# Another order of the weight transfers, and of the first small products, in a fused CIN kernel

## The chip, the cores and the metric

The kernel runs on one core of a Trainium2 chip. The metric is the device time of one execution in microseconds (us), as the median of several runs. The core has five engines that run side by side: TensorE (PE in the profile, PEld its weight loads), VectorE (DVE), ScalarE (ACT), GpSimd (POOL) and SyncE (SP), which only issues transfers. Sixteen DMA engines carry the transfers that ACT, SP and POOL issue.

## The reference

```python
B, F, E = (1024, 39, 64)      # of x as it is given; HID = [64, 64, 64]
def _cin_layer(Xk, X0, W, b):
    O = W.shape[0]
    Hk, Fdim = (Xk.shape[1], X0.shape[1])
    Wr = W.reshape(O, Hk, Fdim)
    return jnp.einsum('bhe,bfe,ohf->boe', Xk, X0, Wr) + b[None, :, None]
X0 = sparse_embedding
Xk = X0
outs = []
for W, b in ((W0, b0), (W1, b1), (W2, b2)):
    Xk = _cin_layer(Xk, X0, W, b)
    outs.append(Xk.sum(axis=-1))
cin_output = jnp.concatenate(outs, axis=-1)
return cin_output @ fc_w.T + fc_b
```

Three layers, each a product of all pairs of fields (39 of x with 39 or 64) with a weight matrix, summed at the end to one number for each of the 1024 rows.

## The kernel before, in words

Only the first layer is computed as it stands. The output needs no more of layers two and three than sums over the embedding axis with fc, and these are linear in the weights. So W2 and the last third of fc are put together into a small matrix V2 (`v2` in the code), and V2 with W1 into a second set of columns beside W0. One big product per block then gives both, and the end result is a product of the two, summed.

**The main loop.** x is cut in 32 blocks of 32 rows (2048 columns). For a block POOL gathers the fields in five arrangements (`roll`, L174) out of a table in DRAM (`xd`), VectorE multiplies pairs of arrangements (`product`, L219, six for a block, and a small one, L221, for two blocks), and TensorE multiplies each by the weights of its chunk (`multiply`, L561; `join`, L581 and L592 for the small one). ScalarE and VectorE finish a block (L604 to L622). VectorE runs four chunks ahead of TensorE.

**The start**, which the change is about, must do two things before that loop:

*Weights.* TensorE turns fc's row into columns, by products of one row with a single one (`turn`, L323): `turn_twice` with a doubled row that POOL writes (`fcrow2`, L320) and `turn_row` straight from fc's row. Both write columns of one PSUM tile, `small`. VectorE makes `fc2` of column 0 (L357). Then on TensorE, in this order: W2 with `fc2` (L403), two small products that double the result (L435, `spread_v2`), seven transposes of W0 (L415, `turn_w0`), and W1 with V2 in four groups (L484). In between VectorE transposes L403's result (L422) and writes V2 (L448, L455). ScalarE copies the turned W0 (L461) into `both`, VectorE transposes L484's four results (L493), and ScalarE and VectorE copy them to `both` as well (L500, L503). From `both`, `weight_rows` takes the sums for one chunk (L526, L528), `weight_turn` transposes them on TensorE (L545) and ScalarE writes them to `wa` (L546, L547), whose columns the main product loads. There are eight chunks; the first four are made before the loop, the rest inside it.

*Rows of x.* The first block doesn't come out of the table: two halves of x are loaded by themselves (`xh`, L252), and eight gathers read them (L389), four arrangements for each half. Behind the sixth POOL issues the load of block 1 (L168). SP copies both halves to the table (L393), and a ninth gather takes the fifth arrangement from there.

**What sets the order.** Each engine runs its instructions in the order in which they are written; there is no scheduler. ACT issues W2, x's first half, W0, W1 and x's second half on its own queue, one behind the other, ahead of all its other work. Between TensorE's products stand spins (`spin`, L279), products of constants that nobody reads; they keep TensorE at work.

Of the kernel before, what the change touches and what calls it, by code (L numbers as in the profile page):

```python
# [60 lines left out]
B, F, E, H = 1024, 39, 64, 64  # L61
# [14 lines left out]
MM = 512  # L76
# [71 lines left out]
def cin_kernel(ctx: ExitStack, tc: tile.TileContext, x, w0t, b0, w1, b1, w2, b2, fc_w, fc_b, out):  # L148
    nc = tc.nc
# [75 lines left out]
    with prep as prep:  # L225
        w2s = prep.tile([128, FH // 2], F32, name="w2s")
        w1s = prep.tile([128, FH // 2], F32, name="w1s")
        w0s = prep.tile([NW * F, NF * H], F32, name="w0s")
        flat = prep.tile([128, 4, NA, 32], F32, name="flat")
        fcrow = prep.tile([1, 3 * H], F32, name="fcrow")  # L230
# [20 lines left out]
        def load_half(k):  # L251
            nc.scalar.dma_start(  # L252
                xh[k].rearrange("f (b e) -> b f e", e=E), x[k * SB : (k + 1) * SB]
            )

        nc.scalar.dma_start(w2s, w2.rearrange("o (s n) -> (o s) n", s=2))
        load_half(0)
        nc.scalar.dma_start(w0s, w0t.rearrange("b (s a) h -> (b s) (a h)", s=NW))
        nc.scalar.dma_start(w1s, w1.rearrange("o (s n) -> (o s) n", s=2))
        load_half(1)  # L260
        nc.gpsimd.iota(place, pattern=[[0, 1]], base=0, channel_multiplier=1)
        nc.gpsimd.iota(apart, pattern=[[1, 128]], base=0, channel_multiplier=-1)
# [14 lines left out]
        def spin(n=1, cols=MM // 2):  # L277
            for _ in range(n):
                nc.tensor.matmul(  # L279
                    idle[:, 0:cols],  # L280
                    nc.const_aps.tensor(1.0, (128, 128), F32),
                    nc.const_aps.tensor(1.0, (128, cols), F32),
                    start=True,
                    stop=True,
                )

        spin(1, MM)


        tmp = prep.tile([128, 16], F32, name="tmp")  # L290
# [31 lines left out]
        def turn(dst, row):  # L322
            nc.tensor.matmul(dst, row, one, start=True, stop=True)  # L323

        def turn_row(h, at, row, k):
            turn(small[h : h + H, at : at + 1], row[:, k * H : k * H + H])

        def turn_twice(at, row, k):
            turn(small[:, at : at + 1], row[:, k].rearrange("p h s -> p (h s)"))
# [6 lines left out]
                nc.gpsimd.memset(steps_by[:, k, i : i + 1], float(by))  # L336
        bothv = both.rearrange("p (a b) -> p a b", b=FT)
        nc.gpsimd.memset(bothv[0:H, :, F], 0.0)
        for at, k in ((0, 1), (6, 0)):
            turn_twice(at, fcrow2, k)  # L340
        spin(1, 3 * MM // 4)

        nc.vector.tensor_copy(row, place)
        step(row, F, 1.0, j)
# [151 lines left out]
        for k, a in groups:  # L496
# [4 lines left out]
            if k > 1:  # L501
# [4 lines left out]
                    ),  # L506
                    flat[0:H, first, new:, 0 : FT - 32],
                )
        spin(1, MM)
        for h in (0, H):  # L510
            turn_row(h, 1, fcrow, 0)
        turn_row(0, 2, fcrow, 2)
        spin(1, MM)
        first = [prods.tile([128, BLK], F32, name="p", tag="p") for _ in range(3)]


# [164 lines left out]
    n, c = steps[3]  # L681
# [9 lines left out]
    for at, (n, c) in enumerate(steps[:-TAIL]):  # L691
# [30 lines left out]
        if at + AHEAD < len(steps):  # L722
            n, c = steps[at + AHEAD]
# [84 lines left out]
```

## Time and profile before

| what | value |
|---|---|
| median of 3 runs | 734.01 us (733.33 to 734.38) |
| the profiled execution, its own time | 733.53 us |
| span of the profile (first to last instruction) | 731.5 us |
| bytes read from HBM, written | 196.76 MB, 10.60 MB |
| main product L561: 1536 passes, busy | 665.2 us |
| first pass of the main product | at 17.40 us of the span |

TensorE takes an f32 product in two passes, so each matmul of the code stands twice in the profile. The times in the timeline count from the start of the span; a group of instructions of one line stands there with the start of its first and the time until its last ends. What a timeline names in brackets is the idle time of that engine ahead of the instruction, and the event that came last before it; with waits for several events it can be another one that ended the wait.

The shares by stage, the first instructions of the weights' and rows' paths and their waits are shown in the prediction.

### The profile page before, as it was taken

How to read it: one execution, taken by the hardware profiler on the slowest of the kernel's cores; microseconds unless marked ns; L12 is line 12 of the kernel's file. 1: busy time of each engine (PE TensorE's matmuls, PEld its weight loads, DVE VectorE, ACT ScalarE, POOL GpSimd, SP SyncE). 2: the span in 40 equal slices, each digit the busy share in tenths (PEclk: the TensorE clock that was granted, in tenths of full speed). 3: DMA queues.
4: the chain of work that ended last, by engine and by line, in shares of the span. 5: the costliest groups of instructions: out<-in, count | busy, mean ns of one | idle time of the engine just before them, and what ended most of it. 6: DMA issues, size and time to landing. Idle time of an engine off the chain costs nothing.

```text
span 731.5 us, 6359 instructions
## 1 busy us (share of the span) xinstructions
PE 726.7 (99%) x2379; PEld 315.3 (43%) x2379; DVE 638.2 (87%) x521; ACT 167.0 (23%) x240; POOL 401.0 (55%) x254
## 2 busy tenths in 40 slices
PE   9999999999999999999999999999999999999998
PEld 4444444444444444444444444444444444444443
DVE  6989699988889988889988889888898988889885
ACT  3332121222212222121222212222121221212222
POOL 6779869636555445754537555455654547545300
PEclk9999999999999999999999999999999999999999
DMA  8986796989575787757679575886767777566700
GB/s 273 378 322 251 304 367 247 382 324 366 219 283 222 284 339 279 277 226 280 273 288 326 230 280 222 310 345 233 280 244 278 299 287 280 197 267 234 288 0 1
DMA packets 65983, 197.24 MB, mean 270 GB/s; under 512 B 40110, under 2 KB 40179, under 8 KB 45984
## 3 DMA queue, kind: packets, MB, share of 16 engines
q0 software_dynamic: 28784, 185.56, 64.9%
q1 hardware_dynamic: 35468, 9.29, 5.5%
q10 hardware_dynamic: 1700, 1.99, 0.9%
q8 instruction: 18, 0.29, 0.2%
q14 instruction: 13, 0.11, 0.0%
HBM read 196.76 MB, written 10.60 MB: 283 GB/s over the span
## 4 chain that ended last, share of the span: by engine, by line
PE 87%; DVE 5%; issue 3%; DMA 2%; POOL 2%; ACT 0%; DVEq 0%; POOLq 0%
PE po L561 80%; PE po L581 4%; DVE p L219 3%; PE po L592 2%; POOL r L174 2%; DVE g L611 1%; DMA r<-xd,lists 1%; DMA b0s<-in_b 1%; PE idle L279 1%; DVE sums L622 1%; DVE pairs L528 0%; PE pv L403 0%; PE pt L484 0%; PE pw L415 0%; PE pv L484 0%
## 5 line engine op out<-in xcount | busy, mean ns | idle before, releaser
L561 PE MATMUL po<-p,wa 128*128 128x512 f32 x1536 | 665.2, 593 | 0.6 <-DVE p L219 0.5
L219 DVE TENSOR_TENSOR p<-r 128x2048 f32<-128x2048 f32 (+2 forms) x198 | 433.8, 2223 | 72.8 <-PE po L561 63.8
L174 POOL DMA_INDIRECT r<-xd,lists x156 | 316.3, 2028 | 264.4 <-issue 255.0
L561 PEld LDWEIGHTS po<-p,wa 128*128 128x128 f32 x1536 | 289.7, 190 | 371.9 <-issue 353.7
L609 ACT ACTIVATE z<-po,columns 64x512 f32<-64x512 f32 x128 | 87.4, 683 | 374.2 <-PE po L592 216.0
L611 DVE SCALAR_TENSOR_TENSOR g<-po,b0s,z 64x512 f32<-64x512 f32 x128 | 95.9, 749 | 9.3 <-ACT z L609 5.3
L604 ACT COPY g<-r 39x1024 f32<-39x1024 f32 x64 | 66.7, 1043 | 161.5 <-DVE sums L622 129.7
L622 DVE TENSOR_REDUCE sums<-g 103x16 f32<-103x1024 f32 x62 | 75.6, 1219 | 2.1
L174 POOL DMA_INDIRECT u<-xd,lists x16 | 40.1, 2509 | 7.1 <-issue 4.6
L581 PE MATMUL po<-p,wa 32*64 32x512 f32 x512 | 31.6, 600 | 0.0
L174 POOL DMA_INDIRECT v<-xd,lists x16 | 26.5, 1659 | 4.9 <-issue 4.9
L221 DVE TENSOR_TENSOR p<-u,v 128x1024 f32<-128x1024 f32 x16 | 19.5, 1216 | 0.0
L581 PEld LDWEIGHTS po<-p,wa 32*64 32x64 f32 x512 | 9.4, 131 | 20.1 <-issue 20.1
L592 PE MATMUL po<-u,wa 32*64 32x512 f32 x256 | 17.0, 587 | 0.0
L174 POOL DMA_INDIRECT r<-xh,lists x8 | 8.0, 1002 | 4.7 <-DVE tmp L384 2.6
L592 PEld LDWEIGHTS po<-u,wa 32*64 32x64 f32 x256 | 5.8, 132 | 8.1 <-issue 8.0
L279 PE MATMUL idle<-const-float32-1.0 128*128 128x512 f32 (+2 forms) x12 | 7.7, 732 | 0.8 <-PEq L795 0.8
L528 DVE TENSOR_TENSOR pairs<-both 128x2 f32<-128x2 f32 (+27 forms) x59 | 6.1, 172 | 0.3
L546 ACT COPY wa<-tr 128x128 f32<-128x128 f32 x8 | 2.1, 266 | 15.3 <-PE tr L545 15.3
L279 PEld LDWEIGHTS idle<-const-float32-1.0 128*128 128x128 f32 x12 | 2.5, 253 | 1.9 <-issue 1.7
L168 POOL DMA_DIRECT2D xd<-in_x x3 | 3.2, 1056 | 0.0
L461 ACT COPY both<-pw 64x468 f32<-64x468 f32 (+2 forms) x4 | 1.9, 472 | 4.4 <-issue 4.3
(97 smaller groups left out, 55.2 us busy)
## 6 DMA issues: line engine op xcount, KB each, us to landing
xd<-in_x SPq DMA_DIRECT2D x28, 312.0 KB
r<-xd,lists POOLq DMA_INDIRECT x156, 9.1
xd<-in_x POOLq DMA_DIRECT2D x3, 312.0 KB
w2s<-in_w ACTq DMA_DIRECT2D x1, 624.0 KB
w1s<-in_w ACTq DMA_DIRECT2D x1, 624.0 KB
w0s<-in_w0t ACTq DMA_DIRECT2D x1, 380.2 KB
xh<-in_x ACTq DMA_DIRECT2D x2, 156.0 KB
xd<-xh SPq DMA_DIRECT2D x2, 156.0 KB
```

The source lines that it names most:

```text
L174: nc.gpsimd.indirect_dma_start(dst, None, table, bass.IndirectOffsetOnAxis(ap=lists[:, k : k + 1], axis=0))
L219: nc.vector.tensor_tensor(p[:, cols], r[:, i, cols], r[:, k, cols], ALU.mult)
L221: nc.vector.tensor_tensor(p[:, 0:SUB], ut[n // 2 % 2], vt[n // 2 % 2], ALU.mult)
L279: nc.tensor.matmul(idle[:, 0:cols], nc.const_aps.tensor(1.0, (128, 128), F32), nc.const_aps.tensor(1.0, (128, cols), F32), start=True, sto ...
L528: nc.vector.tensor_tensor(out, diagonal(a, b, sa, sb), diagonal(b, a, sb, sa), ALU.add)
L561: nc.tensor.matmul(po[n][m], wa[:, c, side : side + 2 * H], p[:, bass.ts(m, MM)], start=n % 2 == 0 and c == 0, stop=n % 2 == 1 and c == NP ...
L581: nc.tensor.matmul(dst[half * H : half * H + H], wa[rows, NPAIR, at : at + H], p[rows, bass.ts(side, MM)], start=t >= 2, stop=t < 2 and ha ...
L592: nc.tensor.matmul(dst[half : half + H], wa[rows, NPAIR + 1, H : 2 * H], ut[n // 2 % 2][rows, bass.ts(side, MM)], start=False, stop=t < 2,)
L604: nc.scalar.copy(gt[H : H + F], rt[n % 2][0:F, 0, bass.ts(m, SUB)])
L609: nc.scalar.activation(z[one], po[n][m][other], AF.Identity, bias=fc0s[other])
L611: return lambda: nc.vector.scalar_tensor_tensor(g[n][m // 2][0:H, at], po[n][m][one], b0s[one], z[one], ALU.add, ALU.mult)
L622: nc.vector.tensor_reduce(sums[:, b_at : b_at + SB], g[n][m // 2].rearrange("p (b e) -> p b e", e=E), AX.X, ALU.add,)
```

## The change

ACT issues its transfers in the order W2, W1, x's first half, W0, x's second half. The first spin has 256 columns instead of 512. All five turns of fc's row now stand ahead of L403: two of `turn_row` that only read fc's row come first, then the two of `turn_twice`, then the last `turn_row`. The spin behind them has 128 columns instead of 384. After L484 the three `turn_row` are gone and the two spins of 512 columns that stood around them come one after the other. In the new kernel lines from about L290 on are numbered differently, by -1 to +3. No other instruction is added or taken away on any engine.

```diff
         nc.scalar.dma_start(w2s, w2.rearrange("o (s n) -> (o s) n", s=2))
+        nc.scalar.dma_start(w1s, w1.rearrange("o (s n) -> (o s) n", s=2))
         load_half(0)
         nc.scalar.dma_start(w0s, w0t.rearrange("b (s a) h -> (b s) (a h)", s=NW))
-        nc.scalar.dma_start(w1s, w1.rearrange("o (s n) -> (o s) n", s=2))
         load_half(1)
...
-        spin(1, MM)
+        spin()
...
+        for h in (0, H):
+            turn_row(h, 1, fcrow, 0)
         for at, k in ((0, 1), (6, 0)):
             turn_twice(at, fcrow2, k)
-        spin(1, 3 * MM // 4)
+        turn_row(0, 2, fcrow, 2)
+        spin(1, MM // 4)
...
-        spin(1, MM)
-        for h in (0, H):
-            turn_row(h, 1, fcrow, 0)
-        turn_row(0, 2, fcrow, 2)
-        spin(1, MM)
+        spin(2, MM)
```

## The prediction

> **What bounds the kernel now.** First the engines' busy time on the page, then stretches of the span, then the timeline of its first 30 us.
>
> ```profile
> PE 726.7 (99%) x2379; PEld 315.3 (43%) x2379; DVE 638.2 (87%) x521; ACT 167.0 (23%) x240; POOL 401.0 (55%) x254
> ```
>
> TensorE is busy 726.7 of 731.5 us. A busy TensorE need not run at its peak, so I went through the starts of its matmuls one after the other: from 20.75 us a 512-column pass starts every 0.43 us up to the end of the main product, and the only later gap over 0.15 us is one of 0.62 us at 101.02. The steady part is TensorE's own and the change leaves it alone. What can move is when the main product (L561) starts, at 17.40, and whether it then stalls.
>
> In this view the columns are stretch, length, busy time of PE, PEld, DVE, ACT, POOL, clock, mean share of the 16 DMA engines, GB/s:
>
> ```profile
> 5.00:9.00 4.00, 4.00 (x13) 1.44 (x14) 2.72 (x17) 1.11 (x2) 1.58 (x2) 1.00 0.93 275
> 9.00:13.00 4.00, 4.00 (x16) 3.15 (x17) 1.61 (x9) 2.21 (x5) 3.09 (x4) 1.00 0.98 278
> 13.00:17.40 4.40, 4.23 (x18) 1.90 (x16) 3.80 (x17) 2.16 (x9) 3.48 (x5) 1.00 0.98 352
> 17.40:30.00 12.60, 12.43 (x31) 5.29 (x32) 12.27 (x42) 4.05 (x15) 8.30 (x6) 1.00 1.01 375
> 30.00:44.00 14.00, 14.00 (x77) 5.80 (x76) 12.26 (x23) 4.37 (x21) 10.50 (x10) 1.00 1.01 391
> ```
>
> The DMA engines are full from about 5 to 44 us. So a transfer here is paid for by every later one, and DMA time lost early is not made up before 44 us. VectorE has 12.27 of 12.60 us in the stretch from 17.40 to 30.
>
> From the timeline (start, duration, then in brackets the idle time before and its releaser):
>
> ```profile
> 5.34 2.40 PE L403 MATMUL pv<-w2s,fc 128*64 128x320 f32 x8
> 7.11 1.05 POOL L174 DMA_INDIRECT r<-xh,lists  x1 [2.60 <-DVE tmp L384]
> 8.82 0.62 PE L435 MATMUL pv<-blocks,twice 64*128 64x20 f32 x4
> 9.38 1.63 PE L415 MATMUL pw<-unit,w0s 117*128 117x117 f32 x7
> 10.79 2.36 PE L484 MATMUL pt<-w1s,v 128*128 128x320 f32 x4
> ...
> 17.40 1.12 PE L561 MATMUL po<-p,wa 128*128 128x512 f32 x2 [0.17 <-issue]
> ...
> 23.06 2.45 DVE L219 TENSOR_TENSOR p<-r 128x1024 f32<-128x1024 f32 x2 [0.32 <-DMA r<-xh,lists]
> ...
> 28.70 0.79 DVE L528 TENSOR_TENSOR pairs<-both 128x22 f32<-128x22 f32 x7
> ...
> 29.66 0.27 PE L545 MATMUL tr<-unit,pairs 128*128 128x128 f32 x1
> ```
>
> The trace's semaphore records say when each transfer of ACT's queue had landed: W2 4.78, x's first half (xh0) 6.24, W0 8.69, W1 9.94, x's second half (xh1) about 10.1. Against these:
> - POOL's first gather is put down to "DVE tmp L384", but POOL's own wait on xh0 ends at 6.27 and the gather starts 0.84 later: xh0 is what it waits for. The next seven follow at some 1.24 us each.
> - At 23.06 DVE waits 0.32 for gathered rows, those of L389's seventh gather, landed at 23.04.
> - From there DVE has no gap until its sums for the fifth chunk end at 29.50, and the transpose waiting for them loads at 29.55, which is just when TensorE is ready for it. So 23.04 is on the path already, with about 0.1 us of slack.
> - W0 (8.69) is ready before L415 (9.38), and W1 (9.94) before L484 (10.79): neither is waited for.
>
> **What the skill says.** The Trainium skill, "DMA: Bandwidth & Descriptors", section "Queues, rings and completion order", says each DMA engine takes the descriptors of one issuer's ring in ring order. The trace agrees: the landings above are in issue order. "Issuing engines are not separate DMA queues" on the same page says that transfers from ACT, SP and POOL share the 16 engines; here POOL's gathers show it by taking 4.6 us from start to landing for the first and 7.2 us for the fifth to seventh, as the engines fill. "TensorE: Matmul & The Clock Gate", "What's actually happening", says that TensorE starts at half clock and is let go after a busy window of about 3.4 us whose phase is not tied to the kernel. Here passes of L484 start 0.53 us apart up to 12.95 and 0.29 to 0.33 apart after it, so the clock came at about 13.0.
>
> **The change, part by part.**
>
> 1. *W1 ahead of xh0, W0 and xh1.* ACT's five issues (0.41, 0.63, 0.83, 0.36, 0.55 us) only change places, and end at 3.65 as before. W1 lands some 3 us earlier, at about 6.6, and nobody gains: L484 stands behind L415 on TensorE, whose order is unchanged. W1 is 128 packets of 4,992 B at 0.19 to 0.24 us, on 16 engines 8 x 0.21 = 1.7 us. That goes ahead of xh0: 6.24 + 1.7 = 7.9, and ahead of W0.
>
> 2. *W0.* Its last data packet ended at 7.85, and W1 then took the engines to 9.48. In the new order W0 ends where W1 did, 9.3 to 9.5; its semaphore came 0.46 (W1) to 0.84 us (W0) after the last data, so it lands at 9.8 to 10.3. L415 moves from 9.38 to about 9.9 to 10.4, and with it L484, the transposes of its result, the weights and the start of L561: +0.5 to +1.0, I take 0.7.
>
> 3. *The gathers.* First gather at 7.9 + 0.9 = 8.8 instead of 7.11, so +1.7 for all eight and for the load that POOL issues among them at 14.38. On the DMA engines: the first gathered packet came 1.8 us after issue (8.9), so now about 10.6. ACT's transfers, which shared their last 1.2 us with 64 gather packets of 0.16 us (64 x 0.16 / 16 = 0.64 us, up to 0.8 with their longer packets), end at about 9.35 instead of 10.08. The engines so stand idle from 9.35 to 10.6, 1.25 us. A gather is 128 x 0.16 / 16 = 1.27 us of engine time against 1.24 us of issue: nothing catches up. The seventh gather lands at 23.04 + 1.25 = 24.3. SP's copies of x to the table wait for xh1, which is no later, and cost the same time in either order. Bounds: 0.5 (SP's copies, issued at about 9.8, fill part of the hole) and 1.7 (the shift in issue).
>
> 4. *fc's products first.* TensorE loses a spin of 512 columns to one of 256, and one of 384 to 128. At half clock (0.85 us per 512-column pass, two passes) that is 0.85 + 0.85 us, and the three turns that come in cost 0.2 us a pass at this clock, six passes of which the first two pairs lie side by side: about 0.8 us. They read fcrow, landed at 1.99. The turns of fcrow2 still wait for POOL (2.78), and behind them stand one turn and the short spin, to about 4.5; L403 then waits for W2, 4.78, and starts at about 4.87, 0.47 before 5.34. fc2 (DVE L357, 3.87) may now come up to 0.4 us later and is still ready by 4.5. V2 and L435 so come 0.47 earlier, at 8.35, and L415 stands waiting for W0 a whole us: nothing is gained. The cover is W0. If W0 were there, it would be worth those 0.47 us.
>
> 5. *The turns taken out near 15.2* (three, 15.10 to 15.42 with the gap around them): they lie between spins, ahead of a transpose that waits for DVE's sums (16.35). Nothing. The copies of small to columns come at 17.35, far behind.
>
> Sum. Path by weights: everything to DVE's product at 21.52 is 0.7 later, so DVE would be free for its next at 23.45. Path by gathers: rows at 24.3. The second is later and takes the first in: DVE restarts 1.25 us late, its sums end at 30.75 instead of 29.50, and the transpose takes off the slack of 0.1: TensorE is 1.15 late at 29.66, and stays so, as nothing behind it waits. At 101.02 the 0.62 us gap hangs on a gather of POOL, which is behind by as much as TensorE; I add 0.05. Total +1.2 us: the profiled execution of 733.53 (span 731.5, 2.0 around it) would be 734.7. It stands 0.5 below the median of the runs, 734.01, so 735.2 for a median.
>
> **Rivals.**
> - *A, the sum above: the hole in the DMA engines decides.* 735.2, by its bounds (0.5 and 1.7) 734.5 to 735.8. For it: no slack at 23.06 and at 29.55, full DMA engines. Against: some 0.5 us of idle DMA could be filled by others. Chance 0.55.
> - *B, TensorE's clock comes late.* TensorE now stands for about 1 us before L415 and has 0.5 us less of full-width work before it. If the window that ends at 13.0 doesn't count as busy, the clock comes 3.4 us later by the skill's window, and L484's last four passes cost 0.53 instead of 0.29: 4 x 0.24 = 1.0 on top of 0.7, so the weights' path is 1.7 late and beats the gathers' 1.15; with W0 at its upper bound 2.0, and with a first us of L561 at half clock 2.5. 735.9 (735.4 to 736.8). For it: the clock came only after the window 9.6 to 13.0, and not after the one before, which held small matmuls and a gap. Against: from 9.9 on the stream is as dense as before. Chance 0.24.
> - *C, not slower: the DMA engines hide the reordering.* If xh0 lands by about 6.5 (W1's packets running into the time in which the engines now wait for memory, share 0.62 over the first 5 us) and W0 by 8.4, the gathers' landing doesn't move and V2 comes 0.47 earlier. It decides where the hole is under 0.1 us. Then -0.3 (the gathers at 23.04 hold part back): 733.7, 733.0 to 734.3. For it: TensorE does start L403 earlier, and gathers wait in a long queue anyway (7.2 us). Against: ring order, and a TensorE that still runs W0 before W1. A gain of more needs a clock a whole window earlier. Chance 0.21.
>
> **How the numbers follow.** 0.2%, 1.5 us, is about what a measurement of this kernel can tell from no change; slower begins at 735.5. Of A's 0.55 some 0.24 lies above it, of B's 0.24 some 0.21: slower 0.45. Faster (below 732.5) needs more than C has, and keeps 0.09 of C for what I haven't seen. Same: 0.46. The range leaves out a little of C below and of B above: 733.5 to 736.8. A alone: 734.5 to 735.8.
>
> **What would show it.** In the profile after: L415 preceded by idle time of TensorE of near 1 us and starting near 10; the first gather near 8.8; L403 near 4.9; the DMA share between 9 and 11 us low; DVE waiting for gathered rows ahead of L219 over 1 us near 24; the gap on TensorE before a transpose near 30. It is wrong if the first gather keeps its place near 7.1, or if L415 starts by 9, or if the passes of L484 are at 0.53 us to their end (B).

## The result, and the profile after

The changed kernel takes 735.96 us (median of 9 runs, 733.31 to 737.78) against 733.99 (9 runs, 733.27 to 734.84): 1.0027 times the time before, 95% interval 1.0018 to 1.0037. In two later series, each on a chip of its own, it was 1.0042 (1.0024 to 1.0060) and 1.0005 (0.9993 to 1.0017). So it is slower in two series and not distinguishable from before in a third. A ratio is not the quotient of the two medians here and below, and can differ from it by up to 0.0021.

The profiled execution is the fastest of the nine, 733.31 us, and its span is the same 731.5 us as before's. The mechanism can be read in it; the size in the median can't. The same stretches as before (length, busy time of PE, PEld, DVE, ACT, POOL, clock, DMA share, GB/s):

```profile
5.00:9.00 4.00, 4.00 (x15) 1.80 (x16) 2.88 (x19) 1.41 (x3) 0.53 (x1) 1.00 0.73 231
9.00:13.00 4.00, 4.00 (x13) 2.99 (x13) 1.83 (x10) 2.34 (x5) 3.08 (x4) 1.00 0.61 197
13.00:17.40 4.40, 3.94 (x12) 1.94 (x11) 3.40 (x16) 2.16 (x9) 3.48 (x5) 1.00 0.91 325
17.40:30.00 12.60, 12.26 (x29) 4.72 (x29) 11.63 (x40) 3.88 (x12) 9.85 (x7) 1.00 0.99 353
```

Between 9 and 13 us the DMA engines' share (the mean of their busy time) is 0.61 where it was 0.98: that is the hole which the prediction spoke of. VectorE has 11.63 us of work from 17.40 to 30 where it had 12.27. From the changed kernel's timeline (start, duration, idle time before and its releaser; the L numbers are those of the new kernel):

```profile
4.86 2.40 PE L406 MATMUL pv<-w2s,fc 128*64 128x320 f32 x8
...
8.34 0.62 PE L438 MATMUL pv<-blocks,twice 64*128 64x20 f32 x4
...
8.47 1.05 POOL L174 DMA_INDIRECT r<-xh,lists  x1 [3.96 <-DVE tmp L306]
...
8.89 1.63 PE L418 MATMUL pw<-unit,w0s 117*128 117x117 f32 x7
...
10.31 2.36 PE L487 MATMUL pt<-w1s,v 128*128 128x320 f32 x4
...
17.26 1.13 PE L560 MATMUL po<-p,wa 128*128 128x512 f32 x2
...
22.02 1.23 DVE L219 TENSOR_TENSOR p<-r 128x1024 f32<-128x1024 f32 x1 [0.33 <-DMA r<-xh,lists]
23.88 2.46 DVE L219 TENSOR_TENSOR p<-r 128x1024 f32<-128x1024 f32 x2 [0.63 <-DMA r<-xh,lists]
...
30.35 0.33 PE L544 MATMUL tr<-unit,pairs 128*128 128x128 f32 x1 [0.44 <-DVE pairs L527]
```

The last line is what the change costs in this execution: TensorE stands still for 0.44 us before the transpose that was at 29.66 and is now at 30.35, waiting for VectorE's sums, which are late because VectorE waited 0.33 and 0.63 us for gathered rows. I call it the fifth transpose of weights below. Side by side, from the two traces (landings from their semaphore records):

| us | before | changed |
|---|---|---|
| W2, xh0, W0, W1, xh1 landed | 4.78, 6.24, 8.69, 9.94, 10.1 | 4.72, 7.60, 8.71, 6.25, 9.3 |
| last packet of ACT's transfers, first of the gathers | 10.1, 8.9 | 9.0, 10.2 |
| first gather starts, seventh has landed | 7.11, 23.04 | 8.47, 23.85 |
| full clock granted to TensorE | 13.02 | 13.84 |
| first pass of the main product | 17.40 | 17.26 |
| fifth transpose | 29.66 | 30.35 |
| gap of TensorE at 101 | 0.62 | none |
| last pass of the main product | 725.78 | 725.80 |

The 0.69 us lost at 30 and the 0.62 us not lost at 101 cancel, and so the two spans agree. The question for the experiments was therefore threefold: which of the two parts of the change is slower, whether it is the gathers, and what the gap at 101 is.

### The profile page after: what moved, and what is told of

Its sections match the earlier page's. It is cut to its first block, busy times and chain, and to the rows that moved or that the text cites. A ratio compares the mean times of both kernels' runs of the same rounds, so it can differ in the third digit from the quotient of the medians.

```text
span 731.5 us, 6359 instructions
## 1 busy us (share of the span) xinstructions
PE 725.9 (99%) x2379; PEld 316.1 (43%) x2379; DVE 638.4 (87%) x521; ACT 166.9 (23%) x240; POOL 390.8 (53%) x254
## 4 chain that ended last, share of the span: by engine, by line
PE 96%; DVE 1%; POOL 1%; DMA 1%; issue 1%; ACT 0%; DVEq 0%
PE po L560 89%; PE po L580 4%; PE po L591 2%; DMA r<-xh,lists 1%; POOL r L174 1%; DVE p L219 1%; PE pv L406 0%; DVE pairs L527 0%; PE small L323 0%; DVE g L610 0%; PE idle L279 0%; DVE sums L632 0%; ACT z L608 0%; PE tr L544 0%; POOL shifts L315 0%
## 5 line engine op out<-in xcount | busy, mean ns | idle before, releaser
L174 POOL DMA_INDIRECT u<-xd,lists x16 | 27.4, 1712 | 5.8 <-issue 4.3
L279 PE MATMUL idle<-const-float32-1.0 128*128 128x256 f32 (+2 forms) x12 | 5.7, 580 | 0.8 <-PEq L794 0.8
L544 PE MATMUL tr<-unit,pairs 128*128 128x128 f32 x8 | 2.3, 286 | 1.1 <-DVE pairs L527 1.1
```

The costliest lines, as they stand in the source:

```text
L174: nc.gpsimd.indirect_dma_start(dst, None, table, bass.IndirectOffsetOnAxis(ap=lists[:, k : k + 1], axis=0))
L279: nc.tensor.matmul(idle[:, 0:cols], nc.const_aps.tensor(1.0, (128, 128), F32), nc.const_aps.tensor(1.0, (128, cols), F32), start=True, sto ...
```

## The experiments

Two theories at first, called G and K in the expectations. G: W1 holds up xh0, the gathers come late, VectorE and then TensorE wait for them. K: TensorE's clock comes later or less surely, since less full-width work stands ahead of L403.

**The changed kernel again**, with no edit.

> The changed kernel once more, for a second trace and more times. Two theories. G (gathers): W1 holds up the first half of x, the gathers come late, VectorE waits, and TensorE stalls some 0.6 us before the transpose near 30 us; the rest of the difference to before is chance. K (clock): TensorE's full clock is granted at a moment that varies more than before, since less dense work stands ahead of L406, and the executions in which it comes late (after 13.8 us, the one of the first profile) are the slow ones. G expects nearly all runs within 1 us of 734.6. K expects 735 to 736 as median, runs spread over 3 us or more, and, if the trace falls on an execution above 735, passes of L487 at 0.53 us to their end and some passes of L560 near 0.86 us instead of 0.43.

Measured: 735.35 us (734.11 to 739.73, 8 runs) against 733.80 for before on this chip (35 runs), ratio 1.0042 (1.0024 to 1.0060; the quotient of the medians is 1.0021). G had nearly all runs within 1 us of 734.6, and five of the eight are. The spread of 5.6 us and the median are K's, but on this chip before's own runs spread over 7.0 us (731.31 to 738.27), so the spread tells nothing. And the clock is not the cause: in this trace it was granted at 8.89, five microseconds earlier than in the first, and the time was no better (734.11 for the execution). What TensorE then waits for:

```profile
14.40 0.30 PE L544 MATMUL tr<-unit,pairs 128*128 128x128 f32 x1 [0.46 <-DVE pairs L527]
14.54 0.60 PE L279 MATMUL idle<-const-float32-1.0 128*128 128x256 f32 x2
17.14 1.10 PE L560 MATMUL po<-p,wa 128*128 128x512 f32 x2 [2.00 <-DVE p L219]
...
30.47 0.33 PE L544 MATMUL tr<-unit,pairs 128*128 128x128 f32 x1 [0.53 <-DVE pairs L527]
```

and VectorE, in the same execution:

```profile
16.31 0.69 DVE L219 TENSOR_TENSOR p<-r 128x512 f32<-128x512 f32 x1 [2.05 <-DMA r<-xh,lists]
```

The weights are ready 2.2 us sooner (first transpose at 14.40 instead of 16.61) and nothing comes of it: the very first product waits 2.05 us for the second gather, which landed at 16.21.

**The transfers alone.** The kernel before, with this edit only:

```diff
         nc.scalar.dma_start(w2s, w2.rearrange("o (s n) -> (o s) n", s=2))
+        nc.scalar.dma_start(w1s, w1.rearrange("o (s n) -> (o s) n", s=2))
         load_half(0)
         nc.scalar.dma_start(w0s, w0t.rearrange("b (s a) h -> (b s) (a h)", s=NW))
-        nc.scalar.dma_start(w1s, w1.rearrange("o (s n) -> (o s) n", s=2))
         load_half(1)
```

> The kernel before with the transfers alone in the new order (W2, W1, x's first half, W0, x's second half); TensorE's order and spins as before. G expects the whole difference of the changed kernel, +1.5 to +2 us over before. K expects +0.3 to +0.7 (the stall near 30 us alone), with runs spread no wider than before's 1.6 us. Both expect the first gather near 8.5.

Measured: 735.74 us (733.92 to 736.34, 9 runs), ratio 1.0024 (1.0008 to 1.0041). By the medians that is +1.9, inside what G expects, and as much as the changed kernel's difference on this chip (+1.6). The trace has the same waits as the changed kernel's:

```profile
24.48 2.47 DVE L219 TENSOR_TENSOR p<-r 128x1024 f32<-128x1024 f32 x2 [1.06 <-DMA r<-xh,lists]
...
30.97 0.33 PE L545 MATMUL tr<-unit,pairs 128*128 128x128 f32 x1 [0.41 <-DVE pairs L528]
```

**TensorE's part alone.** The changed kernel with the edit above undone.

> The changed kernel with ACT's transfers in the order of before (W2, x's first half, W0, W1, x's second half); TensorE's products and spins as in the changed one. G expects before's time within 0.4 us (first gather near 7.1, no stall near 30). K expects +1 us or more over before and runs spread over 3 us.

Measured: 733.91 us (731.97 to 737.62, 19 runs), ratio 1.0007 (0.9996 to 1.0017): before's time, as G expects. The spread of over 3 us that K expects is there too, but no wider than before's own on this chip. In its trace the clock came at 8.16, about as early as in the repeat of the changed kernel, and the rows were there:

```profile
13.91 0.69 DVE L219 TENSOR_TENSOR p<-r 128x512 f32<-128x512 f32 x1
...
15.31 1.88 DVE L219 TENSOR_TENSOR p<-r 128x512 f32<-128x512 f32 x3
```

The first product starts at 13.91 with no wait instead of 16.31, and the main product at 14.79 instead of 17.14. But the fifth transpose is at 29.62, only 0.85 earlier, since the seventh gather lands at 23.11: between the two, TensorE waits. An early start alone is worth nothing here.

**Full spins.** The changed kernel with the two spins back at 512 and 384 columns.

> The changed kernel with the two spins at their size of before (512 columns ahead of fc's products, 384 behind them), everything else as changed. G expects the changed kernel's time. K expects the spread to fall to that of before (1.6 us) and the median to +0.3 to +0.9 over before.

Measured: 735.09 us (734.07 to 737.77, 10 runs), ratio 1.0024 (1.0013 to 1.0035). The median is 0.3 below the changed kernel's on that chip and 1.3 above before's, where K has at most 0.9, and the intervals overlap. The fifth transpose is at 30.88, late as in the other traces of the new order. With that, and with a clock that came at 8.89 in the repeat of the changed kernel and gained nothing there, K is out as the main cause.

The next four ran on another chip, on which before itself took 734.90 us with runs from 733.12 to 738.93 (36 runs).

**x's first half back in second place, W1 third.** Against the changed kernel:

```diff
         nc.scalar.dma_start(w2s, w2.rearrange("o (s n) -> (o s) n", s=2))
-        nc.scalar.dma_start(w1s, w1.rearrange("o (s n) -> (o s) n", s=2))
         load_half(0)
+        nc.scalar.dma_start(w1s, w1.rearrange("o (s n) -> (o s) n", s=2))
         nc.scalar.dma_start(w0s, w0t.rearrange("b (s a) h -> (b s) (a h)", s=NW))
```

> The changed kernel with ACT's transfers in the order W2, x's first half, W1, W0, x's second half: W1 still ahead of W0, but x's first half back in its old place. Two theories. G (gathers): the late first half of x is the whole loss; so the first gather starts at 6.3 to 7.2 again, the seventh gather lands near 23.1, the fifth transpose of weights (29.6 before, 30.4 to 31.0 in the changed order) near 29.6, and the time is before's within 0.5 us. W (weights): it is W0 behind W1 that costs; then +0.8 us or more over before remains, and L415 starts after 9.4 with idle time ahead of it.

Measured: 736.34 us (733.45 to 737.76, 12 runs), ratio 1.0006 (0.9985 to 1.0028; 1.0020 by the medians): too wide to decide. In the trace both theories are half right. The first gather is back at 6.25 and the seventh lands at 22.16, as G says. But W0, behind W1 and in its last part beside the gathers, lands at 10.90, the transposes of W0 (L418 here) start at 10.95 after 1.90 us of idle time, and the weights are the later path: fifth transpose 31.86, 9.7 us behind the gather.

**x's first half one place later still**: W2, W1, W0, xh0, xh1.

> The changed kernel with x's first half one place later still: W2, W1, W0, x's first half, x's second half. G expects the first gather near 9.4, the seventh to land at 24.6 to 25.5, the fifth transpose 6.5 us after it (31.1 to 32.0) and +0.7 to +1.2 us over the changed kernel. W expects a gain over the changed kernel, since W0 comes earlier (L415 no later than 8.9).

Measured: 735.93 us (733.99 to 737.54, 12 runs), ratio 0.9998 (0.9983 to 1.0013; 1.0014 by the medians). Both theories had spoken of the changed kernel's time, and that kernel was not run on this chip. In the trace G's numbers come in from the seventh gather on (landed 24.64, fifth transpose 31.16; the first gather, at 8.73, is earlier than G's 9.4), yet the time does not follow. The trace is of the slowest of the twelve executions, and its main product has further gaps, of 1.54 us at 59.33 and 1.69 at 105.28, where before's trace had only the one at 101.02. On this chip the spread of the runs hides a microsecond.

**POOL's load of block 1 behind the eighth gather**, in the kernel before and in the changed one:

```diff
                 gather_rows(rt[0][:, i, cols], xh[k], i)
-                if k and i == 1:
-                    load(1, nc.gpsimd)
+        load(1, nc.gpsimd)
         for k in (1, 0):
             nc.sync.dma_start(xd[0][0:F, halves[k]], xh[k])
```

> The kernel before with POOL's load of block 1 (312 KB, issued between the sixth and the seventh gather) moved behind the eighth gather. G expects the seventh gather to land about 1.0 us earlier (near 22.0), since a load's worth of DMA time is taken from ahead of it, and 0.4 to 1.0 us less than before where TensorE's clock is granted early (by 9 us), nothing where it comes at 13; the gathers of block 1 stay early enough. W expects before's time.

> The changed kernel with the same move of POOL's load. G expects the seventh gather near 22.9 to 23.4 and some 1.0 us less than the changed kernel, so about half of its loss taken back. W expects the changed kernel's time.

Measured: 737.73 us (14 runs), ratio 1.0033 (1.0019 to 1.0048), and 740.45 (7 runs), ratio 1.0064 (1.0038 to 1.0090). Both theories missed. The seventh gather did come earlier (21.57 in the first, 23.44 in the second), but block 1's gathers read what that load brings, and in the second kernel they were not early enough after all:

```profile
44.08 2.29 DVE L219 TENSOR_TENSOR p<-r 128x2048 f32<-128x2048 f32 x1 [6.37 <-DMA r<-xd,lists]
...
46.42 2.08 PE L559 MATMUL po<-p,wa 128*128 128x512 f32 x2 [2.92 <-DVE p L219]
```

and the stretch after it, in the view by stages:

```profile
48.00:53.00 5.00, 5.00 (x8) 1.95 (x7) 4.83 (x3) 0.00 (x0) 3.00 (x2) 0.56 0.46 181
```

VectorE waits 6.37 us for a gather of block 1 and TensorE 2.92 for VectorE. During this wait the granted clock falls to a half, from 45.6 to 52.4, and the passes from 47 to 52 start about 0.86 us apart. In the trace of before with the late load VectorE waits too, 5.00 us, but TensorE doesn't stand still there. What that trace has lost by 30 us begins elsewhere: ScalarE's first copy of turned weights came 1.9 us after the transpose it reads, with nothing in the trace that explains it; this stays open.

A third chip, on which before took 734.48 us (732.24 to 738.36, 67 runs), was for the question whether the gathers' delay alone does it, and how it stands to the variation of the later gaps (theory V in the expectations).

> The changed kernel, as the measure for the other three on the same chip. Two theories. G: the time is the landing of the seventh gather + 6.5 us to the fifth transpose + a constant, with small additions from later gaps; +1.2 to +2.2 us over before. V: the time of the start is drowned by gaps near 59 and 101 to 105 us that differ from execution to execution and from chip to chip; then less than +0.7 us on a chip on which before itself spreads over 5 us, and more only by chance.

Measured: 735.09 us (14 runs), ratio 1.0005 (0.9993 to 1.0017). The trace has G's numbers (seventh gather 23.69, fifth transpose 30.19) and a gap of 0.90 at 101.88. The time is V's: 0.6 us by the medians, though the interval just reaches G's lower end of 1.2.

> The changed kernel with the transfers in the order W2, x's first half, W1, W0, x's second half. G expects the seventh gather at 22.2 to 23.2 and 1 us or more less than the changed kernel, unless W0, now behind W1 and beside the first gathers, lands near 11 and holds L415 and the weights: then the fifth transpose comes later than the gather plus 6.5, and the gain is under 1 us. V expects no difference from the changed kernel beyond 0.7 us.

Measured: 737.97 us (732.16 to 740.29, 22 runs), ratio 1.0033 (1.0017 to 1.0049): slower than the changed kernel by the medians, the case that G had set apart. But the times fall into two groups, seven of them from 732.16 to 734.58 and fifteen from 737.56 up. The trace is of the second group; what the executions of the first did differently isn't in a trace. In it:

```profile
10.15 1.63 PE L418 MATMUL pw<-unit,w0s 117*128 117x117 f32 x7 [1.26 <-DMA w0s<-in_w0t]
...
105.60 2.84 PE L560 MATMUL po<-p,wa 128*128 128x512 f32 x6 [1.68 <-DVE p L219]
```

W0 holds TensorE up at 10.15, the clock came only at 16.18, and the fifth transpose is at 31.40 with rows that landed at 22.84. It also shows the other half of its loss, the gaps behind: 0.56 at 44.61, 1.05 at 59.49, 1.84 at 105.60 (measured as in the table below, from the start of one pass to the next; the view counts 0.16 less).

> The changed kernel with the transfers in the order W2, W1, W0, x's first half, x's second half. G expects +0.3 to +0.9 us over the changed kernel (seventh gather near 24.6, fifth transpose near 31.1). V expects no difference from it beyond 0.7 us, of either sign.

Measured: 735.25 us (733.12 to 738.16, 22 runs), ratio 1.0012 (1.0002 to 1.0022): 0.2 us over the changed kernel, under what G asks and within V's band.

**The gathers alone, late.** The kernel before with one instruction more:

```diff
+        hold = prep.tile([1, 1], F32, name="hold")
+        nc.gpsimd.tensor_copy(hold, w0s[0:1, 0:1])
         halves = [slice(0, SUB), slice(SUB, BLK)]
```

> The kernel before, transfers and TensorE's work as before, with one addition: ahead of the first gather POOL copies one element of W0, so that it waits for W0's landing (8.7 instead of 6.2). This delays the gathers alone, by about 2.4 us. G expects the first gather near 9.5, the seventh to land 1.5 to 2.2 us later than before's 23.1, the fifth transpose 6.5 us behind it and +1.3 to +2.2 us over before, as much as the changed kernel or more. V expects before's time within 0.7 us.

Measured: 735.75 us (734.50 to 738.06, 22 runs), ratio 1.0013 (1.0004 to 1.0022), 1.3 us over before by the medians, at the lower end of G's band; the interval alone, 0.3 to 1.6 us, would leave room for V. Transfers and weights are those of before, and the clock came early (7.55). From the trace:

```profile
8.15 0.18 POOL L387 COPY hold<-w0s 1x1 f32<-1x1 f32 x1 [3.64 <-DMA w0s<-in_w0t]
8.96 1.05 POOL L174 DMA_INDIRECT r<-xh,lists  x1 [0.63 <-DVE tmp L306]
...
25.34 2.49 DVE L219 TENSOR_TENSOR p<-r 128x1024 f32<-128x1024 f32 x2 [1.08 <-DMA r<-xh,lists]
...
31.85 0.33 PE L547 MATMUL tr<-unit,pairs 128*128 128x128 f32 x1 [0.55 <-DVE pairs L530]
```

A late first gather, with nothing else changed, gives the whole pattern: seventh gather 25.32, VectorE waits for it, fifth transpose 6.53 us later. That is 2.2 us later than before's, of which the median shows 1.3.

**The traces in one table.** Late gaps are those of TensorE over 0.13 us behind the fifth transpose, taken from the start of a pass to the start of the next, less the usual 0.43; the remainder is the last pass of the main product less the fifth transpose less these gaps. (Of the twelve experiments the changed kernel with the late load is left out, whose late gaps run into passes at half clock.)

| kernel | clock granted | 7th gather landed | fifth transpose | difference | late gaps | remainder |
|---|---|---|---|---|---|---|
| before | 13.02 | 23.04 | 29.66 | 6.62 | 0.62 | 695.50 |
| TensorE's part alone | 8.16 | 23.11 | 29.62 | 6.51 | 0 | 695.45 |
| changed | 13.84 | 23.85 | 30.35 | 6.50 | 0 | 695.45 |
| changed, again | 8.89 | 23.97 | 30.47 | 6.50 | 0.58 | 695.55 |
| changed, third chip | 12.73 | 23.69 | 30.19 | 6.50 | 0.90 | 695.55 |
| full spins | 8.25 | 24.37 | 30.88 | 6.51 | 0 | 695.44 |
| transfers alone | 7.54 | 24.46 | 30.97 | 6.51 | 0 | 695.45 |
| x late | 12.53 | 24.64 | 31.16 | 6.52 | 3.23 | 695.64 |
| gathers alone | 7.55 | 25.32 | 31.85 | 6.53 | 0 | 695.44 |
| x late, third chip | 8.44 | 24.44 | 31.96 | 7.52 | 2.51 | 695.65 |
| x second, third chip | 16.18 | 22.84 | 31.40 | 8.56 | 3.45 | 695.51 |
| x second | 15.92 | 22.16 | 31.86 | 9.70 | 1.04 | 695.50 |
| before, late load | 12.91 | 21.57 | 32.22 | 10.65 | 1.74 | 695.60 |

In nine rows the fifth transpose is 6.5 us behind the seventh gather (6.62 in before), whenever the clock came: the rows come last. In the last four something else does: the eighth gather, which landed only at 26.70, then twice the weights that waited for W0, then ScalarE's late copy. What follows the transpose is 695.4 to 695.7 us in all of them, plus late gaps. So the end is the later of two paths at 30 us plus those gaps. The first of these is shown to move with the change: 23.04 and 23.11 with the old order of transfers, 23.69 to 24.46 with the new. The second differs from trace to trace of one kernel (0, 0.58 and 0.90 for the changed one).

What the gap at 101 is can be followed back in the traces. Eight of the fourteen have a gap of 0.58 to 1.98 us between 101 and 106. In each of these eight VectorE had waited 5.36 to 5.48 us for gathered rows, at 82.55 to 87.09, and after one or two shorter waits it worked on without a pause and was late when TensorE came to need its product. In the other six VectorE's longest wait between 68 and 92 us was 2.09 to 3.60 us, and there is no gap. In before:

```profile
82.55 2.29 DVE L219 TENSOR_TENSOR p<-r 128x2048 f32<-128x2048 f32 x1 [5.36 <-DMA r<-xd,lists]
```

In the changed kernel:

```profile
81.56 2.29 DVE L219 TENSOR_TENSOR p<-r 128x2048 f32<-128x2048 f32 x1 [3.60 <-DMA r<-xd,lists]
```

Kernels with the old and with the new order of transfers are in both groups, and the changed kernel itself is in both. So the change doesn't settle whether an execution has this gap; what does stays open.

## Why the prediction was right, and where it was off

It forecast +1.2 us by a hole in the DMA engines' work. +1.97 was measured, inside its range (733.5 to 736.8), though the 735.96 is just above the range that it gave for this hole alone (734.5 to 735.8), and inside that of rival B. So the time alone doesn't speak for the mechanism; the experiments do. That the number came so near is in part luck: the start lost 0.69 us in the profiled execution, not the 1.15 forecast for TensorE at that point, and the rest of the +1.97 is not in that trace.

- *The path (part 3) holds.* The gathers' first start came at 8.47 (forecast 8.8), VectorE waited for the seventh at 23.88 (24.3), TensorE stood before the fifth transpose at 30.35 (30.8). The transfers alone give 1.0024, TensorE's part alone 1.0007 with an interval that holds 1, and the delay of the gathers alone makes the same pattern.
- *The hole was right, what it costs was not quite.* From ACT's last packet to the first gather's it is 8.96 to 10.22, 1.26 us, as forecast (1.25, from 9.35 to 10.6); SP's copies did not fill it, their first data came at 11.80. But the landing of the seventh gather moved by 0.81 in the first trace, and by 0.65 to 1.42 in all five traces of the new order. "Nothing catches up" fits three of the five: from the first gathered packet to the seventh landing it took 14.10 to 14.25 us there, against 14.14 in before. In the changed kernel's first two traces it took 13.63 and 13.80, so there 0.3 to 0.5 us were caught up. What makes the difference was not found. One thing that the sum held fixed is seen to move: the same 1698 packets of ACT's queue took 6.92 us of the sixteen engines' time in before and 5.98 to 6.19 in the five; W1's took 0.238 us (median) in its old place and 0.192 in the new. So the busy share of the DMA engines was no fixed measure of what they could move.
- *W0 (part 2) was wrong.* It was to land at 9.8 to 10.3 and to hold L415 up to about 10; it landed at 8.71 and L415 (L418 in the new kernel) started at 8.89, with no idle time ahead of it. By the prediction's own list a start by 9 was a sign that it is wrong, and for this part it is. I read W1 as taking the engines after W0's last packet (7.85 to 9.48), and so let W0 end where W1 had ended. In fact 92 of W1's 128 packets had started before 7.85: the transfers land in the order of their issue, but one doesn't wait for the end of the one before. In the new order W1's last packet ended at 5.91 and W0's at 8.40, only 0.55 later than before. With x second the forecast's times do come true: W0's last packet ended at 9.42 and 10.02, it landed at 10.11 and 10.90, and L418 waited (1.26 and 1.90 us). There W1's packets ran on to 8.26 and 8.49; why they take so much longer behind x's first half than ahead of it was not shown.
- *fc's products (part 4): size right, cover wrong.* L403 came 0.48 earlier (0.47 forecast), and L484 too, 10.31 instead of 10.79, since W0 did not eat it. Yet the first weights were no earlier (first transpose 16.61 against 16.50): the full clock came 0.82 later, and L484's passes ran at 0.53 us nearly to their end, which the prediction had named as the sign of rival B. And where the clock came early, the rows ate it.
- *Rival B (clock) has its mechanism, but not the effect given.* The grant moved from 7.54 to 16.18 between traces, by 5 us for the same kernel, which agrees with the Trainium skill's "TensorE: Matmul & The Clock Gate", "What's actually happening": its window is not tied to the kernel's start. But three traces of the changed kernel with grants at 8.89, 12.73 and 13.84 have the fifth transpose within 0.28 us, and TensorE's part alone with its grant at 8.16 has it where before has it with 13.02.
- *Rival C (not slower)* needed W0 by 8.4 and xh0 by 6.5. W0 nearly was there (8.71), xh0 was not (7.60). On the third chip the time alone can't exclude it.

The kept traces of the changed kernel show +0.5 to +0.8 us at the fifth transpose, the medians of two series +1.6 and +2.0. What the rest of the runs lost is not in a trace: those kept were in the faster half of their runs (the fastest of nine, the fastest of eight, the fourth of fourteen). The later gaps are a candidate: in other orders, in traces of slow executions (with x late, the slowest of twelve and the twentieth of 22), they add up to 3.23 and 2.51 us. That the change makes them more frequent was not shown.

## What to carry to other kernels

At the start of a kernel, ask of every transfer what stands behind it in its queue, and issue first the one whose user has the longest chain still to go; here that is x for the gathers, not W1, whose user waits for two other things anyway. W1 ahead of W0 alone was no gain either, since then W0's user waits. An engine that gets its input earlier gains nothing if the other input of the next step comes later: follow both paths to where they meet before moving either. Transfers that land in order can still run side by side, as W0 and W1 did here; look at when each one's packets start before adding their times up. And when two profiles have the same span, compare them event by event before believing that nothing has changed.

## What the runs showed of the hardware

- The clock can fall back when TensorE waits for its rows. In the trace of the transfers alone it waited 1.86 us (17.01, nothing but spins and one transpose behind it), and the clock was at a half from 17.78 to 21.19, 3.41 us, though passes ran the whole time; the 3.41 us before that, from 14.37, hold the wait. The main product's first pass with the wait ahead of it:

```profile
17.01 1.29 PE L561 MATMUL po<-p,wa 128*128 128x512 f32 x2 [1.86 <-DVE p L219]
```

  and the stretch after it, in the columns of the stages above:

```profile
17.80:21.20 3.40, 3.40 (x6) 1.43 (x6) 3.40 (x14) 0.38 (x2) 2.79 (x3) 0.50 1.03 397
```

  It cost nothing that lasts, since the rows were the later path: the fifth transpose is still 6.51 us behind the gather. A wait is not enough, though: the changed kernel again waited 2.00 us before 17.14 and kept its clock. One thing separates the two in the fourteen traces. Ahead of the end of the main product the clock fell seven times, each time a whole multiple of 3.41 us after it had been granted (6.83, 10.24 or 23.89). In the last 3.41 us ahead of such a fall TensorE had been idle for 1.75 to 2.84 us in all (1.75, 1.79, 1.86, 1.87, 2.10, 2.21, 2.84). In the stretches of this length, counted from the grant, behind which the clock stayed, the largest idle time is 1.61 us, in the changed kernel again, whose wait lay across the border of two of them.
- An earlier first gather did not bring the seventh forward here. With TensorE's part alone the first gather started at 6.34 instead of 7.11, and the seventh landed at 23.11 instead of 23.04.
- Three series gave 1.0027, 1.0042 and 1.0005 for the same pair of kernels, and before's own runs spread over 1.6 us in the first (9 runs), 5.8, 6.1 and 7.0 in the others (36, 67 and 35). A change of a quarter of a per cent needs more than one series and more than one chip.
